# A two-branch cross-attention kernel on one core: the list scheduler's durations, switch penalties and ranks set anew

## The chip, the cores and the metric

The kernel runs on one core of a Trainium2 chip. A core has a matrix engine (TensorE, PE in the profile), a vector engine (DVE), an activation engine (ACT), a general engine (GpSimd, POOL) and an engine that here issues transfers only (SyncE, SP). Each works through its own list of instructions in order; they wait for one another by semaphores. The metric is the device time of one execution in microseconds. The kernel before took 582.35 us, the median of three runs (582.03 to 583.09).

## The reference, cut to what matters

```python
# x (2, 2048, 640) float32, ctx_768 (2, 128, 384); 8 heads of 80; the last T = 4 context rows are "ca"
query = x @ Wq;  keyt = enc @ Wk;  valt = enc @ Wv         # enc: the other 124 context rows
hs = _mha(query, keyt, valt)                               # text branch
ca_q1 = einsum('btc,th->bch', ca, Wq_ca)[:, indices, :]    # 2048 rows picked from 384
ca_hs1 = _mha(ca_q1, x, x)                                 # adapter: 384 distinct queries over 2048 rows
ca_q2 = ca_hs1 @ Wq
ca_hs2 = _mha(ca_q2, ca @ Wk_ca, ca @ Wv_ca)
out = (hs + ca_hs2) @ Wout + b_out + x
```

## The kernel before, in words

*Two branches.* The text branch makes the queries q of 512 rows of x at a time (eight blocks: four for each of two batches), the scores sc against the 124 keys, a softmax (row maximum m on DVE, exponential p with its row sum on ACT, a reciprocal r, the product p<-p,r), a transposition in blocks (eb on DVE, a store kept<-eb to device memory and four loads pT<-kept), then the products ph with the values (copied to hs), and po with Wout, which DVE adds to the rows of x (x_more, last_rows). It does this in 16 units (m) of 256 rows. The adapter branch makes, for each batch, small products of x (pyz, copied to yz, turned into y and zop), the first scores s1 (24 products of four row tiles into the one score buffer of four banks, each followed by a maximum mx on DVE), a shift of the queries by these maxima (mt, cop), the second scores s2 (24 products, each followed by an exponential ea on ACT), the contraction acc of ea with y, its normalisation (accs, prod, the second small softmax p2) and the product po with w_sb into 384 rows o2 in device memory. At the end of a unit each of its two row tiles gets its o2 rows added by an indirect DMA on POOL (`add_second`) and is stored. Products by Strassen-like sums (x_sums, wq_sums, wout_sums, sums of hs) save matmuls at the price of additions on DVE and POOL.

*Tilings of PE.* A matmul may use part of the array: column tiles (128*32 in the profile, four beside one another), row tiles for the scores s (32*128), halves for sc (64*128), quarters for pyz (64*32), and the whole array for transposes and the set-up (128*128). `matmul` is line 210 of the profile, `by_columns` 222, `transpose` 230, the operations of the other engines 245, `dma` 265; all operations go through these helpers, so the groups are known by tile names.

*The planner.* The order is not written out. Each piece of the kernel is a generator (`softmax`, `adapter`, `probabilities`, `chain` inside `text_out`, and so on) that yields `Do` entries: an engine (or several to choose from, `EITHER`), what must be done first, buffers it needs (`Room`) and frees, a rank, and a tiling mode. `Desk.run` keeps a clock of its own while the program is built: for every engine it finds the earliest time at which an entry could start, takes among the entries of that time the one with the lowest rank plus penalty for changing PE's tiling, issues it, and adds its assumed duration. `Desk.pin` then keeps that order on each engine in the finished program. So durations, penalties and ranks decide only two things: the order on each engine, and the engine of an operation that may go to several (copies to ACT or DVE; p<-p,r to POOL, DVE or ACT; sums of x, hs and wout to DVE or POOL). `RANKS` adds a number to the rank of single generators, by name and count. `MORE`, `START`, `DRAIN`, `TAIL` and the third argument of each `dma` call are assumed durations in microseconds. Column-tile products are entered as the whole array (`mode=(P, P)`), scores without a mode.

*Events and counters.* Some buffers are given back by counting the users that are done (`used`, `counted`, `scored`, `left`), at the moment when the planner issues the last. The output has a path for rows that are done before o2 is there (`stored`: a part to device memory and back, with the room `ending`); in the program that is built, no row takes that path, and 30 stores of whole rows and four of halves end the kernel.

Of the kernel before, what the change touches and what calls it, by code (L numbers as in the profile page):

```python
# [14 lines left out]
P = 128  # L15
# [49 lines left out]
class Desk:  # L65
# [4 lines left out]
    WHOLE, SWITCH, LEAVE, ANOTHER = (P, P), 328.5, 9.9, 185.7  # L70
    START = {(P, P): 0.107, (64, P): 0.143, (P, 64): 0.107, (64, 32): 0.1, (P, 32): 0.03}
    DRAIN = {
        ((P, P), (32, P)): 0.136, ((P, P), (64, P)): 0.035, ((P, P), (P, 64)): 0.056, ((P, P), (P, 32)): 0.067,
        ((32, P), (P, 32)): 0.049, ((P, 64), (P, P)): 0.07, ((P, P), (P, P)): 0.0,
    }
    DRAINS = {(64, P): 0.172, (32, P): 0.108, (P, 32): 0.115}
    MORE = {
        "v_transpose": 0.025, "v_stream_shuffle": 0.09, "v_scalar_tensor_tensor": 0.07, "v_reciprocal": 0.035,
        "a_activation": 0.045,
    }  # L80
    COLD = 5.2
    TAIL = {"PE": 0.25, "DVE": 0.18, "ACT": 0.2, "POOL": 0.25, "SP": 0.1, "NONE": 0.0}
# [3 lines left out]
        "adapter": {0: 1, 1: 2},  # L86
        "chain": {2: 8, 4: -11, 5: 7, 6: -2, 8: -11, 11: -4, 14: 11, 15: 16, 19: -14, 24: -4, 25: 3, 30: 3.1,
            32: 4, 34: 10, 36: 2, 41: 0.5, 42: 1, 43: 0.5, 44: -10, 45: -10, 48: -8, 50: -5, 51: -5, 52: 7,
            54: 10, 55: 10, 56: 10, 68: -4, 76: -3, 81: 2, 86: 2, 87: 3},
        "contract": {0: 5, 1: 4.5, 2: 8, 3: 8},  # L90
        "halves_away": {1: -4, 2: -2, 4: 4, 6: 6},
        "keys": {0: -10},
        "probabilities": {3: -8, 5: -4, 8: 12, 9: -3, 10: -2, 12: 6, 13: 6, 15: 7},
        "queries_fast": {0: 5, 3: 4},
        "rest_back": {1: 11, 4: 5, 7: 8, 9: 9, 10: 5, 14: 2},
        "second": {0: 2.3},
        "softmax": {0: 5, 2: -7, 3: 6.2, 4: -4, 7: -11, 8: 2, 10: -5, 12: -20, 14: -3, 17: 9, 20: -2, 21: 7,
            22: 7, 25: -5, 29: 2, 30: 6},
        "sums_of_wq": {0: 5.7},
        "text_scores": {0: -8, 1: 3.4, 12: 9},  # L100
        "values_weights": {0: -18},
        "x_load": {1: 4.2, 4: 5},
        "y_rows": {2: 2, 3: 6, 4: 4},
        "y_weights": {0: 1},
        "yz_block": {2: 16, 5: 3.5, 6: 5},
    }

    def __init__(self, tc):
        self.tc, self.nc, self.now, self.spent, self.mode = tc, tc.nc, 0.0, 0.0, None
        self.free = {e: 0.0 for e in self.ENGINES}  # L110
        self.queue = {e: [] for e in self.ENGINES}
        self.events, self.landed, self.channel, self.log, self.begun = {}, 0.0, 0.0, [], {}

# [29 lines left out]
    def change(self, mode):  # L143


        if mode is None or mode == self.mode:
            return 0.0
        return self.LEAVE if self.mode == self.WHOLE else self.SWITCH if mode == self.WHOLE else self.ANOTHER
# [17 lines left out]
    def run(self):  # L166
        while any(self.queue.values()):
            best = None
            for e in self.ENGINES:
                found = [(max(r, self.free[e], self.now), op) for op in self.queue[e] if (r := self.ready(op)) is not None]  # L170
                if found:
                    t = min(x[0] for x in found)
                    t, op = min(
                        (x for x in found if x[0] <= t + 1e-9),
                        key=lambda x: self.order(x[1]) + self.change(x[1].mode),
                    )
                    if best is None or t < best[0]:
                        best = t, e, op
# [23 lines left out]
    def _mode(self, rows, cols):  # L202
        mode = tuple(32 if n <= 32 else 64 if n <= 64 else 128 for n in (rows, cols))
        if mode != self.mode or self.idle:
            self.spent += self.START.get(mode, 0.0)
            self.spent += self.DRAIN.get((self.mode, mode), self.DRAINS.get(self.mode, 0.1))
        self.mode, self.idle = mode, False

    def matmul(self, out, lhsT, rhs, **kw):
        self.pin(self.nc.tensor.matmul(out, lhsT, rhs, **kw))  # L210
        n = 1
        for size in rhs.shape[1:]:
            n *= size
# [3 lines left out]
        self.spent += self.slow() * (1 if one else 2) * max(n / 1.2, 107) / 1e3 / at_once  # L217

    def by_columns(self, out, lhsT, rhs, **kw):
# [3 lines left out]
        n = 1  # L223
        for size in rhs.shape[1:]:
            n *= size
        self._mode(P, P)
        self.spent += 2 * max(n / 1.2, 107) / 1e3

    def transpose(self, out, in_, ident):
        self.pin(self.nc.tensor.transpose(out, in_, ident))  # L230
        self._mode(P, P)
        self.spent += self.slow() * 0.115
# [30 lines left out]
    def dma(self, out, in_, us, issue=0.45, more=2.8):  # L263

        self.pin(self.nc.sync.dma_start(out, in_))
        self.spent += issue
        self.channel = max(self.channel, self.now + self.spent) + us
        self.landed = self.channel + more


@with_exitstack
def kernel(
# [56 lines left out]
    ending, early, late = Room(1), Room(0), {}  # L329
# [570 lines left out]
    def keys():  # L900
# [39 lines left out]
        for i in range(2):  # L940
            op = yield Do(
                "SP", lambda i=i: dma(away[:, :, i].rearrange("e p n -> p e n"), z.bitcast(F32), 0.8), rank=-1,
            )
        for u in range(2):
            for e in range(2):

                def back(u=u, e=e):
                    dma(
                        parts[VH * u + G * e : VH * u + G * (e + 1)],
                        away[e, VH * u : VH * (u + 1)].rearrange("(g d) i n -> (d i) g n", g=4), 0.4,  # L950
# [37 lines left out]
    def load_wout():  # L988

        by_head = Wout.rearrange("(c j d) n -> j d c n", c=4, j=2)  # L990
        for j in range(2):
            yield Do(
                "SP", lambda j=j: dma(wout_sb[VH * j : VH * (j + 1), :4, :], by_head[j, :VH], 2.5),
# [3 lines left out]
        def last():  # L997
            for h in range(HEADS):
                dma(wout_sb[VR * h : VR * (h + 1), 4, :], Wout[D * h + VH : D * (h + 1), :], 0.15)
# [126 lines left out]
    def x_load(b, sb, after):  # L1126
# [8 lines left out]
        for i in range(4):  # L1135
# [3 lines left out]
            def of_pairs():  # L1139
                d1 = VR + (R * i + VH) % P  # L1140
                dma(most[part, :2], v[:, 0::2, :, d0 : d0 + R], 2.2, 1.3)
# [4 lines left out]
            def between_pairs():  # L1146
                if i:
                    g = (0, 2, 1, 3)[i]
                    dma(rest[part], w[:, :, D2 * g - VR : D2 * g + VR], 0.6, 0.6)
                else:  # L1150
                    dma(rest[part, :, :VR], w[:, :, H - VR :], 0.6, 0.6)
                    dma(rest[part, :, VR:], w[:, :, :VR], 0.6, 0.6)
# [26 lines left out]
    def queries(n, after, first=False):  # L1179
# [8 lines left out]
        if first:  # L1188
# [53 lines left out]
            used(b, sb, op)  # L1242
            yield Do("NONE", lambda: None, [("qc", n, j, h) for j in range(2) for h in range(2)], marks=[("q", n)])
            return
        for c in range(NCH):
# [10 lines left out]
            op = yield Do("PE", part, [*after, "wq4"], needs=[(banks, 1), *own], mode=(P, P))  # L1256
            pq, s, q = op.value, op.slots[0][0], q_of[n][0]

            for i0, i1 in ((2, 4), (4, NCH)):
# [5 lines left out]
                op = yield Do("PE", part, mode=(P, P))  # L1265
# [4 lines left out]
        used(b, sb, op)  # L1270
# [6 lines left out]
    def sums_of_wq():  # L1277
# [3 lines left out]
        yield Do("NONE", lambda: None, ["late"])  # L1281
# [39 lines left out]
    def queries_fast(n, after):  # L1321

        sb = divmod(n, NSB)
        yield Do("NONE", lambda: None, after + ["late"])
# [12 lines left out]
        left = {"all": 9, "sums": 4}  # L1337
        rank = 10 + 2 * n

        def counted(op, of_sums):  # L1340
            left["all"] -= 1
            left["sums"] -= of_sums
            if of_sums and not left["sums"]:
                if n + 1 < len(blocks):
                    sums.at[0] = op.at.t
                else:
                    desk.event("last sums").t = op.at.t
            if not left["all"]:
                used(*sb, op)
                if n + 1 == len(blocks):  # L1350
                    desk.event("last query").t = op.at.t

        def chain(c, steps):

            po, s, at = None, None, []
            for k, ((x, y, plus), ready, (i, u)) in enumerate(steps):
# [20 lines left out]
                if x is not None:  # L1377
                    needs = ([(banks, 1)] if k == 0 else []) + ([(qslots, 1)] if n not in q_of else [])
                    op = yield Do("PE", product, ready + at, needs=needs, mode=(P, P))
# [7 lines left out]
                if plus:  # L1387
                    op = yield Do("PE", fifth, [op.at] + at, mode=(P, P))
                counted(op, any(key[0] == "xs" for key in ready))
# [21 lines left out]
        yield from plain(n, t, NCH - 1, rank - 0.5, counted)  # L1411
# [8 lines left out]
    def plain(n, t, c, rank, counted):  # L1420
# [7 lines left out]
        op = yield Do("PE", part, needs=[(banks, 1)], mode=(P, P), rank=rank)  # L1428
        pq, s = op.value, op.slots[0][0]
        for i0, i1 in ((2, 4), (4, NCH)):  # L1430
# [5 lines left out]
            op = yield Do("PE", part, mode=(P, P), rank=rank)  # L1436
        counted(op, False)
        yield Fork(halves_away(n, pq, s, op.at), 0)

    users = {}  # L1440
# [953 lines left out]
```

## Time and profile before

| | |
|---|---|
| median of three runs | 582.35 us |
| profiled execution, its device time | 581.8 us |
| its span | 580.1 us |
| PE busy | 570.3 us (98%) |
| DVE busy | 391.7 us (68%) |
| ACT busy | 309.8 us (53%) |
| POOL busy | 141.6 us (24%) |
| DMA moved | 112.71 MB |
| granted clock of PE | 1.000 |

Spans and starts are those of the one profiled execution. In a list of groups a line gives the helper's line, the engine, the operation, the tiles out<-in, the number of instructions, then busy us and the mean ns of one, then the idle time of that engine just before them. Instructions overlap a little on PE, DVE and ACT: start-to-start is shorter than the recorded duration. In the slices each digit is a tenth of 14.5 us.

### The profile page before, as it was taken

Reading aid. Unit: us, or ns where it says so; the run is one execution under the profiler, and the core shown is the slowest. Engines: PE = TensorE matmul, PEld = TensorE weight load, DVE = VectorE, ACT = ScalarE, POOL = GpSimd, SP = SyncE. Lnnn points to the kernel's source line nnn. Section 1 sums busy time; section 2 is a strip of 40 time slices with the busy share of each in tenths; the row PEclk is TensorE's granted clock in tenths of the full one; section 3 lists DMA queues with packets and bytes.
Section 4 is the critical chain, followed back from the end, with each engine's and each line's share of the span. In section 5 each row is a group of like instructions: output and inputs, shape, how many; then the busy total and the mean of one; then the engine's idle time right before and its main releaser. Section 6 shows DMA issues by size and latency. Waiting matters only on the chain.

```text
span 580.1 us, 19105 instructions
## 1 busy us (share of the span) xinstructions
PE 570.3 (98%) x8115; PEld 308.4 (53%) x8115; DVE 391.7 (68%) x645; ACT 309.8 (53%) x869; POOL 141.6 (24%) x200
## 2 busy tenths in 40 slices
PE   9999999999999999999999999999999999999997
PEld 8885334555555545455455445454455545545453
DVE  2446799999999756356999999973455253444443
ACT  2413376686566898689847447277877613002020
POOL 9102112012206411120114326050140312403241
PEclk9999999999999999999999999999999999999999
DMA  8897866979766888234999969999549487799995
GB/s 245 196 263 131 199 94 187 179 201 172 182 184 137 217 157 221 82 113 149 219 284 247 230 152 236 270 227 275 142 105 266 112 211 155 181 263 247 250 249 139
DMA packets 153039, 112.71 MB, mean 194 GB/s; under 512 B 83701, under 2 KB 126581, under 8 KB 152954
## 3 DMA queue, kind: packets, MB, share of 16 engines
q1 hardware_dynamic: 147322, 100.80, 67.5%
q0 software_dynamic: 5632, 10.69, 11.3%
q8 instruction: 64, 1.05, 0.8%
q14 instruction: 21, 0.17, 0.1%
HBM read 71.23 MB, written 40.22 MB: 192 GB/s over the span
## 4 chain that ended last, share of the span: by engine, by line
PE 64%; DVE 16%; DMA 8%; ACT 6%; issue 4%; SPq 1%; DVEq 0%; ACTq 0%
PE po L222 25%; PE pq L222 9%; PE ph L210 6%; DVE mx L245 6%; PE acc L210 5%; PE s L210 4%; PE pq L210 4%; PE sc L210 3%; ACT ea L245 3%; DMA kept<-eb 3%; DMA pT<-kept 2%; ACT p L245 2%; DVE m L245 2%; DVE q L245 2%; DVE eb L245 2%
## 5 line engine op out<-in xcount | busy, mean ns | idle before, releaser
L245 DVE TENSOR_REDUCE mx<-s 128x4 f32<-128x2048 f32 x48 | 109.4, 2280 | 4.1 <-PE s L210 4.1
L245 ACT ACTIVATE ea<-s 128x2048 f32<-128x2048 f32 x48 | 91.0, 1897 | 24.2 <-PE s L210 23.9
L245 ACT ACTIVATE p<-sc,m 128x124 f32<-128x124 f32 x256 | 90.2, 383 | 10.2 <-DVE m L245 9.7
L222 PE MATMUL po<-wout_sums,hs 128*32 128x320 f32 x1024 | 77.3, 433 | 0.0
L222 PE MATMUL po<-wout_sb,hs 128*32 128x320 f32 x960 | 74.2, 433 | 0.7 <-DVE x_more L245 0.7
L222 PE MATMUL pq<-xt,wq_sb 128*32 128x256 f32 (+1 forms) x928 | 66.3, 418 | 0.5 <-DVE mt L245 0.5
L245 DVE TENSOR_TENSOR x_more<-x_more,po 128x320 f32<-128x320 f32 x72 | 34.3, 483 | 45.5 <-PE po L222 45.4
L2129 POOL DMA_INDIRECT x_more<-o,query x18 | 27.9, 1550 | 124.3 <-DVE x_more L245 92.5
L245 ACT ACTIVATION_READ_ACCUMULATOR p<-sc,m 128x1 f32 x256 | 57.8, 226 | 0.0
L245 ACT COPY hs<-ph 128x512 f32<-128x512 f32 (+1 forms) x34 | 18.5, 551 | 65.8 <-PE ph L210 65.2
L222 PEld LDWEIGHTS po<-wout_sums,hs 128*32 128x32 f32 x1024 | 32.9, 110 | 34.1 <-issue 1.8
L210 PE MATMUL acc<-ea,y_sb 128*32 128x384 f32 (+2 forms) x768 | 51.0, 385 | 0.0
L222 PEld LDWEIGHTS po<-wout_sb,hs 128*32 128x32 f32 x960 | 30.4, 110 | 33.1 <-issue 1.5
L245 DVE TENSOR_REDUCE m<-sc 128x4 f32<-128x496 f32 x64 | 40.0, 662 | 10.4 <-PE sc L210 10.4
L245 DVE TENSOR_TENSOR last_rows<-last_rows,po 128x320 f32<-128x320 f32 x56 | 26.7, 481 | 27.9 <-PE po L222 27.5
L210 PE MATMUL ph<-pT,vpad 128*32 128x256 f32 x768 | 45.3, 380 | 0.1
L245 POOL TENSOR_TENSOR p<-p,r 128x992 f32<-128x992 f32 x8 | 14.8, 1846 | 125.0 <-DVE r L245 125.0
L222 PEld LDWEIGHTS pq<-xt,wq_sb 128*32 128x32 f32 x928 | 27.8, 109 | 29.6 <-issue 13.5
L245 DVE STREAM_TRANSPOSE eb<-p 128x1024 f32<-128x1024 f32 x32 | 39.4, 1233 | 5.6 <-DMA kept<-eb 5.5
L210 PEld LDWEIGHTS sc<-kmain,q 64*128 64x128 f32 x512 | 32.1, 187 | 13.7 <-issue 5.5
L210 PE MATMUL sc<-kmain,q 64*128 64x124 f32 x512 | 38.4, 285 | 0.2 <-ACT p L245 0.2
L245 ACT CAST rests<-landing 128x512 fp32r<-128x512 f32 x30 | 18.7, 635 | 36.2 <-PE sc L210 28.0
(216 smaller groups left out, 847.6 us busy)
## 6 DMA issues: line engine op xcount, KB each, us to landing
kept<-eb SPq DMA_DIRECT2D x32, 512.0 KB, 3.8
pT<-kept SPq DMA_DIRECT2D x64, 256.0 KB, 8.2
landing<-away SPq DMA_DIRECT2D x60, 128.0 KB, 4.3
xi<-in_x_dram SPq DMA_DIRECT2D x56, 128.0 KB, 4.6
x_more<-in_x_dram SPq DMA_DIRECT2D x18, 320.0 KB, 6.8
out_dram<-x_more SPq DMA_DIRECT2D x16, 320.0 KB, 6.6
last_rows<-in_x_dram SPq DMA_DIRECT2D x14, 320.0 KB, 7.2
out_dram<-last_rows SPq DMA_DIRECT2D x14, 320.0 KB, 10.0
```

The costliest lines, as they stand in the source:

```text
L210: self.pin(self.nc.tensor.matmul(out, lhsT, rhs, **kw))
L222: self.pin(self.nc.tensor.matmul(out[j : j + 32], lhsT[:, j : j + 32], rhs, **kw))
L245: self.pin(getattr(engine, what)(*args, **kw))
L2129: desk.pin(nc.gpsimd.indirect_dma_start(out=t, out_offset=None, in_=o2_of[b], in_offset=bass.IndirectOffsetOnAxis(ap=query[:, st : st + 1] ...
```

## The change

All of it lies in the planner and in the bookkeeping that feeds it; each operation computes what it did. The penalties for changing the tiling now depend on both modes (`CHANGE`; letters b for column tiles, s for row tiles of the scores, c for sc, y for pyz, w for the whole array), and column tiles and scores are entered with their own modes. The price of a PE stretch is set by `ENTER`, `EXIT` and `streamed`. An entry that could start later than the earliest one carries a penalty `IDLE`; `AHEAD` (0) is the width of that choice. A transfer now takes one of eight places in flight per queue in the planner (`SLOTS`, `transfer`): a ninth is issued when the first has landed. Each `dma` call has a new assumed duration, and some a new issue time and latency. Buffers are given back by events (`free_x`, `free_q`, `done`, `sum`, `chain` marks) in place of counters. The path over device memory for early rows is gone. `RANKS` grows from some 60 entries to several hundred.

```diff
-    WHOLE, SWITCH, LEAVE, ANOTHER = (P, P), 328.5, 9.9, 185.7
-    START = {(P, P): 0.107, (64, P): 0.143, (P, 64): 0.107, (64, 32): 0.1, (P, 32): 0.03}
...
+    KINDS = {(P, 32): "b", (32, P): "s", (64, P): "c", (64, 32): "y", (P, P): "w"}
+    CHANGE = {
+        "bs": -2.82893e+09, "bc": 34.1, "by": 7.8, "bw": 66.5, "sb": 2.7632e+10, "sc": 659476, "sy": 6.8, "sw":
+        16.2, "cb": 486.2, "cs": 12, "cy": 3.3, "cw": 21.1, "yb": 609.7, "ys": 0.8, "yc": 12, "yw": 9.2, "wb":
+        6379.5, "ws": 14.8, "wc": 27.3, "wy": 16.5,
     }
-    DRAINS = {(64, P): 0.172, (32, P): 0.108, (P, 32): 0.115}
+    AHEAD, IDLE = 0, 214.8
+    ENTER = {(P, P): 0.104, (64, P): 0.143, (64, 32): 0.16, (P, 32): 0.024, (32, P): 0.006}
+    EXIT = {(P, P): 0.07, (P, 32): 0.114}
+    SLOTS = 8
...
-    TAIL = {"PE": 0.25, "DVE": 0.18, "ACT": 0.2, "POOL": 0.25, "SP": 0.1, "NONE": 0.0}
+    TAIL = {"PE": 0.235, "DVE": 0.14, "ACT": 0.145, "POOL": 0.16, "SP": 0.1, "NONE": 0.0}
...
     RANKS = {
-        "adapter": {0: 1, 1: 2},
...
+        "adapter": {0: 37.7, 1: 41.7, 3: 1},
...
-                    t = min(x[0] for x in found)
+                    first = min(x[0] for x in found)
+                    ahead = self.AHEAD if e == "PE" else 1e-9
                     t, op = min(
-                        (x for x in found if x[0] <= t + 1e-9),
-                        key=lambda x: self.order(x[1]) + self.change(x[1].mode),
+                        (x for x in found if x[0] <= first + ahead),
+                        key=lambda x: self.order(x[1]) + self.change(x[1].mode) + self.IDLE * (x[0] - first),
                     )
...
+    def streamed(self, rhs):
+        n = 1
+        for size in rhs.shape[1:]:
             n *= size
+        return (max(n / 1.2, 106 if self.mode[1] > 32 else 27) + (9 if self.mode == (64, P) else 2.5)) / 1e3
...
-        self._mode(P, P)
-        self.spent += 2 * max(n / 1.2, 107) / 1e3
+        self._mode(P, 32)
+        self.spent += 2 * self.streamed(rhs)
...
-    def dma(self, out, in_, us, issue=0.45, more=2.8):
+    def dma(self, out, in_, us, issue=0.47, more=3.0):
 
         self.pin(self.nc.sync.dma_start(out, in_))
-        self.spent += issue
+        self.transfer("SP", us, issue, more)
+
+    def transfer(self, side, us, issue, more=3.0):
+
+        flights = self.flights[side]
+        self.spent = max(self.spent, flights.pop(0) - self.now) + issue
         self.channel = max(self.channel, self.now + self.spent) + us
         self.landed = self.channel + more
+        flights.append(self.landed)
...
-                    op = yield Do("PE", scores, [("zop", b, sb, u), c_at], needs=[(quad, 1)])
+                    op = yield Do("PE", scores, [("zop", b, sb, u), c_at], needs=[(quad, 1)], mode=(32, P))
...
-                lambda: dma(pT[R * j : R * (j + 1)].rearrange("p i k h a -> p i (k h a)"), by_keys[j], 1.1),
+                lambda: dma(pT[R * j : R * (j + 1)].rearrange("p i k h a -> p i (k h a)"), by_keys[j], 1.2, 0.48),
...
-                "SP", lambda: dma(o2_of[b][ct * P : (ct + 1) * P, :], o2, 1.3),
+                "SP", lambda: dma(o2_of[b][ct * P : (ct + 1) * P, :], o2, 1.1, 0.39),
...
-        desk.spent += 1.9
-        desk.landed = desk.now + desk.spent + 6.5
+        desk.transfer("POOL", 1.5, 1.57)
...
-            part = hbm.tile([P, H], F32, tag=f"early_{m}_{k}", name=f"early_{b}_{st}")
-            op = yield Do("SP", lambda: dma(part, t, 1.3), both, frees=[(rows, i)])
...
+        op = yield Do("POOL", lambda: add_second(t, b, st), [*both, ("o2", b), "query"])
+        yield Do("SP", lambda: dma(rows_out, t, 1.3, 0.41), frees=[(rows, i)])
```

More of the change, by code (lines that the diff above doesn't have):

```diff
@@ L1255, in queries @@
             own = [(qslots, 1)] if n not in q_of else []
-            op = yield Do("PE", part, [*after, "wq4"], needs=[(banks, 1), *own], mode=(P, P))
+            op = yield Do("PE", part, [*after, "wq4"], needs=[(banks, 1), *own], mode=(P, 32))
             pq, s, q = op.value, op.slots[0][0], q_of[n][0]
@@ L1323, in queries_fast @@
         sb = divmod(n, NSB)
-        yield Do("NONE", lambda: None, after + ["late"])
+        yield Do("NONE", lambda: None, after + ["late", "wq sums"])
         t, _ = xt[sb]
@@ L2265, in chain @@
-                tile_left[m, i] = tile_left.get((m, i), 4) - 1
-                ends.setdefault((m, i), []).append(op.at)
-                if not tile_left[m, i]:
-                    yield Fork(stored(m, i, ends[m, i]), 1)
+        reads = {(i, u): [] for i in range(2) for u in range(2)}
+        for n, steps in enumerate(chains):
+            for _, _, (place,) in steps:
+                reads[place].append(("sum", m, *place, n))
+        yield Fork(one(Do(
+            "NONE", lambda: None, [("chain", m, n) for n in range(len(chains))], frees=[(hss, at_hs)]
+        )), 0)
```

274 lines of the change are left out of this document (139 added, 135 removed), and 14 rows, old and new, of the table RANKS.

## The prediction

> **What bounds the kernel now.** I read the page first, then the busy times by stretch, then what TensorE (PE) waited for. The page:
>
> ```profile
> PE 570.3 (98%) x8115; PEld 308.4 (53%) x8115; DVE 391.7 (68%) x645; ACT 309.8 (53%) x869; POOL 141.6 (24%) x200
> ...
> PE   9999999999999999999999999999999999999997
> ...
> DVE  2446799999999756356999999973455253444443
> ACT  2413376686566898689847447277877613002020
> ...
> PEclk9999999999999999999999999999999999999999
> ```
>
> PE is busy in every slice and its granted clock never drops. DVE is full twice (slices 5 to 13 and 20 to 24), ACT nearly so between them and around slice 28. The span is 580.1 us and the profiled run 581.8, so 1.7 us lie around it; that run is 0.55 us under the median of 582.35. The busy time of the engines in stretches (stretch, length, then PE, PEld, DVE, ACT, POOL, clock, DMA share, GB/s):
>
> ```profile
> 20.00:110.00 90.00, 89.97 (x931) 50.02 (x932) 68.84 (x121) 40.33 (x131) 11.59 (x41) 1.00 0.79 168
> 110.00:190.00 80.00, 79.02 (x1218) 43.33 (x1214) 77.68 (x103) 55.47 (x212) 21.19 (x24) 1.00 0.76 175
> 190.00:290.00 100.00, 97.64 (x1523) 51.65 (x1519) 62.62 (x102) 83.88 (x201) 15.91 (x16) 1.00 0.66 166
> 290.00:345.00 55.00, 53.96 (x799) 27.84 (x795) 53.88 (x59) 29.82 (x114) 16.25 (x14) 1.00 0.91 234
> 345.00:410.00 65.00, 64.47 (x974) 32.62 (x966) 47.87 (x69) 38.78 (x103) 21.14 (x19) 1.00 0.97 246
> 410.00:470.00 60.00, 59.97 (x952) 31.57 (x945) 28.05 (x56) 42.29 (x75) 10.75 (x12) 1.00 0.63 153
> 470.00:580.10 110.10, 106.38 (x1643) 54.32 (x1642) 45.99 (x99) 13.85 (x28) 29.25 (x19) 1.00 0.86 213
> ```
>
> PE stands idle 0.98 + 2.36 + 1.04 + 0.53 = 4.9 us between 110 and 410 us, and almost nothing at 20 to 110 and 410 to 470. The last 3.72 us are the final addition and stores. So a reordering can win those 4.9 us, the price of PE's changes of tiling, and what is hidden inside "busy". What PE waited for (us, times, longest):
>
> ```profile
> PE s L210 <- ACT ea L245: 1.6, 6, 0.5
> PE unread L210 <- DVE zeros L245: 1.1, 1, 1.1
> PE s L210 <- DVE mx L245: 0.8, 2, 0.5
> PE po L222 <- DVE x_more L245: 0.7, 2, 0.5
> PE pq L222 <- DVE mt L245: 0.5, 1, 0.5
> ```
>
> The largest are the second scores s, which wait until ACT has taken the exponential ea out of the one score buffer, and the first scores, which wait for DVE's maximum mx.
>
> **The change, part by part.** The arithmetic stays: both programs issue the same 4520 matmuls, so PE's streaming costs the same and has no term. What moves is the order on each engine, and which engine takes the operations that two or three may take. Counts of the new program are read from its issue order; their durations are the rows of before.
>
> *Changes of tiling.* The planner adds a penalty to an operation that would change PE's tiling, and the change sets these penalties anew. Stretches of equal tiling go from 270 to 267; those that leave the column tiling (128*32), from 112 to 109. Other kinds keep their numbers. One such departure:
>
> ```profile
> 35.40 1.08 PE L210 MATMUL pa<-first_rows,blk_k 128*32 128x128 f32 x32
> 36.30 0.40 PE L210 MATMUL pa<-wqT,blk_k 128*32 128x128 f32 x8
> 36.63 1.16 PE L210 MATMUL pa<-first_rows,blk_k 128*128 128x128 f32 x8
> ```
>
> Eight groups of four take 36.30 - 35.40 = 0.90 us, 0.1125 each. Two more would end at 36.525; the next tiling starts at 36.63, so leaving cost 0.105 us here (0.137 over all departures that I could place like this). Three fewer: 3 x 0.137 = -0.4 us. Bounds: 0 and -0.4.
>
> *Stages.* For each stage I compared PE's work without waiting with the work of the engine that limits it, start to start. The rows:
>
> ```profile
> L245 DVE TENSOR_REDUCE mx<-s 128x4 f32<-128x2048 f32 x48 | 109.4, 2280 | 4.1 <-PE s L210 4.1
> L245 ACT ACTIVATE ea<-s 128x2048 f32<-128x2048 f32 x48 | 91.0, 1897 | 24.2 <-PE s L210 23.9
> ...
> L245 DVE TENSOR_TENSOR x_more<-x_more,po 128x320 f32<-128x320 f32 x72 | 34.3, 483 | 45.5 <-PE po L222 45.4
> ...
> L245 DVE TENSOR_REDUCE m<-sc 128x4 f32<-128x496 f32 x64 | 40.0, 662 | 10.4 <-PE sc L210 10.4
> ...
> L245 DVE STREAM_TRANSPOSE eb<-p 128x1024 f32<-128x1024 f32 x32 | 39.4, 1233 | 5.6 <-DMA kept<-eb 5.5
> ```
>
> ```profile
> 310.94 2.28 DVE L245 TENSOR_REDUCE mx<-s 128x4 f32<-128x2048 f32 x1
> 313.14 1.24 DVE L245 STREAM_TRANSPOSE eb<-p 128x1024 f32<-128x1024 f32 x1
> ```
>
> ```profile
> 198.25 0.36 ACT L245 ACTIVATE p<-sc,m 128x124 f32<-128x124 f32 x1
> ...
> 198.59 0.36 ACT L245 ACTIVATE p<-sc,m 128x124 f32<-128x124 f32 x1
> ```
>
> A full DVE starts the next instruction 0.08 us before the recorded end (310.94 + 2.28 - 313.14), so I take 0.08 off each; an exponential p with its read-out costs ACT 0.34.
>
> Stage A, the first scores of batch 0 (to about 167 us). DVE's 140 instructions make 120.1 us beside 118.6 of PE; after, 137 make 117.6 beside 115.4. The excess goes from 1.5 to 2.2 us. Read alone, +0.7; the bound below is that all 0.98 of its idle time goes. I take 0: stages overlap, so an excess of this size can move out of the stage.
>
> Stage B, the second scores of batch 0 (181 to 264 us). ACT has 74.5 us beside 82.9 of PE; after, 85.0 beside 92.2. The room shrinks from 8.4 to 7.2 us in a longer stage, as 24 more of the normalisations p<-p,r go to ACT in all (104 to 128, that is three units more). But the score loop gets looser: a score buffer is free again 1.9 us plus two hand-overs after a product, so the other PE work between two second-score products should be about 2.2 us or more. Of the 47 gaps, those below 2.2 us go from 8 to 3, those below 2.55 from 16 to 7. With PE's 1.6 us of waits for ea spread over six places, I take a third to a half of them gone, -0.6. Bounds: -2.4 (the idle time of 190 to 290 gone) and +1.2 (if ACT does all its work as soon as its inputs are there, its worst lateness goes from 1.04 to 2.22).
>
> Stage C, the first scores of batch 1 (266 to 357 us). DVE has 93.1 us beside 91.2 of PE: 24 mx x 2.20 = 52.8, 16 m x 0.58 = 9.3, 24 additions to rows x 0.40 = 9.6, 8 eb x 1.15 = 9.2, and 12.2 of others. After, it has 100.7 beside 101.6: seven more additions and three copies of hs, but 10.4 us more of PE products, so an excess of 1.9 becomes a room of 0.9. The idle time of 290 to 410, 1.04 + 0.53, holds x_more's 0.7 and one mx. I take -1.3; bounds -1.6 and 0.
>
> *Transfers.* The planner now lets a ninth transfer of a queue wait for the first's landing; the chip is given no wait, only another order. Reuse of the output rows in the tail loosens (shortest distance 28 to 33 us), and one stall of the chain below, x_more's, hangs on such a load. -0.3; bounds -0.7 and 0. One place tightens. The pT of unit 0 is now issued on SP right behind the store o<-o, which waits for ACT's copy of a product; from that product to the first ph that needs this pT lie 10.4 us of PE work (16.1 at the tightest place before). The rows of such a group, of its landing, and two links of the chain of waits:
>
> ```profile
> 308.26 0.34 SPq L265 DMA_DIRECT2D o<-o  x1
> ...
> 309.54 1.84 SPq L265 DMA_DIRECT2D pT<-kept  x4
> ```
>
> ```profile
> DMA to landing us min/median/max: 3.5/8.2/11.5
> ```
>
> ```profile
> 316.64 8.04 DMA x_more<-in_x_dram
> 324.69 5.86 DMA pT<-kept
> ```
>
> The copy came about 1.2 us after its product. With 1.2 + 0.4 for the store, some 1.4 to the fourth issue of 1.84, and 8.2 to land, pT is there 11.2 us after the product: 0.8 late. Behind SP's waiting entry queue the loads after it, with ten us of cover each. I take +0.5 (PE's own small waits lengthen the cover); bounds 0 and 4.1 (landing 11.5).
>
> *Other moves.* Five copies of hs and two or three of q go from ACT to DVE where DVE is at four tenths to half busy (slices 25 to 33), so at nothing: in the second scores of batch 1 (369 to 445 us) DVE has 31.8 us of work beside 75.7 of PE. Without that cover a copy would cost the 0.69 us of its row less 0.08. Three sums of hs go from DVE to POOL, and in stage A POOL takes five instead of three of the p<-p,r. Rows that bear on these:
>
> ```profile
> L245 DVE TENSOR_TENSOR x_sums<-xt x3: 676/677/1741, 74.8 to 254.9; 128x512 f32<-128x512 f32 x3
> ```
>
> ```profile
> L245 DVE COPY hs<-ph x4: 640/686/693, 381.1 to 432.1; 128x512 f32<-128x512 f32 x4
> ```
>
> ```profile
> L245 POOL TENSOR_TENSOR p<-p,r x8: 1845/1846/1848, 95.2 to 309.9; 128x992 f32<-128x992 f32 x8
> ```
>
> DVE's sum of two rows takes 677 ns, but once 1741, so two-input work on DVE can stretch by 1.06 us; POOL's product never stretched. I price the two moved products at 0: POOL is a quarter busy and p is needed late. If each of the two held up DVE once in stage A, that is +2.1 us. The Trainium skill says, in "SBUF — State Buffer", section "Who interferes with whom", that a DVE instruction with two SBUF inputs and a GpSimd instruction that reads SBUF share one port pair as an exclusive lock, and the later one waits for the whole of the other; it speaks against these moves. The row of 1741 agrees in sign; the sum by that rule would be 2.1 us higher.
>
> *The sum.* -0.4 + 0 - 0.6 - 1.3 - 0.3 + 0.5 = -2.1 us, so 581.8 - 2.1 = 579.7 on the scale of the profiled run and 580.25 on that of the median. I say 580.0.
>
> **The rivals.** *Nothing but the tiling changes moves.* If DVE and ACT each did all their work as soon as its inputs are there, the latest operand of each stage would be late by amounts that sum to about 4.2 us in both orders; the stalls would then only change places. Against it: the places over 0.25 us late fall from 58 to 34. Then 582.35 - 0.4 = 582.0.
>
> *Most stalls go.* All of 190 to 410's 3.9 us and the switches: 582.35 - 4.3 = 578.0, and with as much again that hides inside "busy" (by the start-to-start of undisturbed products, PE took about 8 us longer there than its streams and tiling changes), down to 574.5. For it: the looser loops. Against: ACT's room in B shrinks.
>
> *Slower: pT of unit 0 lands late.* The cover of 10.4 us less the 3.0 before the last issue leaves 7.4 to land; the case decides at 7.4 plus the 2.6 that the other terms win, a landing of 10.0. At 345 to 410 us transfers take 97% of the DMA engines, and the slowest pT took 11.5; should the new order bring that crowd to 305 us, the stall is 4 to 6 us, and the time 580.0 - 0.5 + 4 to 6 = 583.5 to 585.5. The Trainium skill adds in "TensorE: Matmul & The Clock Gate", Part 1, that about 3.4 us of idle PE sends it to half its clock. No wait of PE in before is over 1.1 us and its clock stays full, so no run here shows that yet.
>
> *Slower: ACT or the shared reads bound A and B.* A at +0.7 in place of 0, B at +1.2 in place of -0.6, and the two products' 2.1: 580.0 + 0.7 + 1.8 + 2.1 = 584.6. For it: stage A has more DVE than PE, so what is lost there isn't hidden. Against: 1741 stands once.
>
> **How the numbers follow.** The forecast 0.42, its own range 578.5 to 581.2; most stalls go 0.17; nothing moves 0.15; pT late 0.13; ACT or shared reads 0.13. Within 0.2% of 582.35 (581.2 to 583.5, what a measurement here can tell from no change) lies the second of these: same 0.15, faster 0.59, slower 0.26. The range 575 to 585 takes in most of every case.
>
> **What would show it.** Right: PE's waits for ea and mx below 1.6 and 0.8 us, for x_more none; idle time at 190 to 290 below 2 us and in stage C near 0. The switches: 109 departures from 128*32. Wrong: a wait of ph for pT near 300 to 320 us over 1 us; DVE sums over 1.5 us in stage A; an idle time of 3 us or more at 180 to 270 us with releaser ea. The forecast falls, too, if landings, which the planner takes as fixed, lengthen in the new order and new waits appear where no term above stands.

## The result, and the profile after

The changed kernel takes 587.73 us (median of five, 585.32 to 588.40); the kernel before, run beside it, 582.03 (five, 581.37 to 583.09). The ratio is 1.0089, with a 95% interval of 1.0064 to 1.0114: it is slower by 0.9%. The profiled execution took 587.91 us with a span of 585.9. One execution of a later run (the maximum first) fell into a slower state, 721.84 us at a mean clock of 0.754, and is left out of that run's median.

The page of the kernel after, its busy times and three of the lines of slices (40 equal slices, tenths busy or, for PEclk, of full clock):

```profile
PE 570.0 (97%) x8115; PEld 309.1 (53%) x8115; DVE 398.6 (68%) x653; ACT 311.2 (53%) x881; POOL 139.2 (24%) x201
...
PE   8999999999989999899999999999999999999997
...
DVE  1456999999798836855699999996633314445343
...
PEclk9999999999989999999999999999999999999999
```

PE's work is the same; PE's busy time and its clock both have a dent in the twelfth slice (161 to 176 us), which the kernel before had not. By stretches (columns as before the change: length, then PE, PEld, DVE, ACT, POOL, clock, DMA share, GB/s):

```profile
0.00:20.00 20.00, 17.71 (x104) 15.88 (x105) 6.14 (x34) 4.75 (x8) 15.48 (x59) 1.00 0.84 260
20.00:110.00 90.00, 90.00 (x915) 50.08 (x917) 69.95 (x130) 36.29 (x111) 12.13 (x41) 1.00 0.82 175
110.00:190.00 80.00, 75.61 (x1130) 40.91 (x1130) 73.51 (x99) 53.81 (x217) 16.88 (x13) 0.98 0.78 174
190.00:290.00 100.00, 97.35 (x1603) 54.71 (x1591) 65.61 (x102) 86.50 (x211) 17.71 (x25) 1.00 0.59 159
290.00:345.00 55.00, 53.03 (x771) 27.67 (x760) 51.77 (x64) 32.12 (x121) 9.65 (x10) 1.00 0.84 232
345.00:410.00 65.00, 64.49 (x950) 33.47 (x946) 58.46 (x77) 37.35 (x131) 23.48 (x21) 1.00 0.88 237
```

PE's idle time at 110 to 190 us went from 0.98 to 4.39 us, and the clock there fell to 0.98, some 1.6 us of 80: together 5.0 us in this one stretch, where the span grew by 5.8 in all. At 190 to 290 the idle time is 2.65 for 2.36, at 290 to 410 it is 2.48 for 1.57. The 2.29 for 1.14 at the start is one late load of x; the runs below that keep this order up to 100 us show 1.13 to 1.16. Against these stands PE's busy time, which includes its changes of tiling: it is 568.1 to 569.1 us in the five later runs whose clock stays at 1.00, and 570.3 before. PE's waits (us, times, longest):

```profile
PE s L266 <- DVE mx L295: 3.4, 3, 2.2
PE s L266 <- ACT ea L295: 2.0, 2, 1.2
...
PE pq L275 <- ACT p L295: 0.8, 1, 0.8
PE pq L275 <- DVE prod L295: 0.7, 1, 0.7
PE s L266 <- DVE zop L295: 0.7, 1, 0.7
```

One wait of 2.2 us for a maximum is new. DVE's instructions ahead of it (start, us, what, and idle time before with its releaser):

```profile
152.94 1.25 DVE L295 STREAM_TRANSPOSE eb<-p 128x1024 f32<-128x1024 f32 x1 [1.05 <-DMA kept<-eb]
...
158.14 0.67 DVE L295 TENSOR_TENSOR q<-q,pq 128x512 f32<-128x512 f32 x1
160.87 1.25 DVE L295 STREAM_TRANSPOSE eb<-p 128x1024 f32<-128x1024 f32 x1 [2.06 <-DMA kept<-eb]
162.31 0.01 DVE L295 LOAD_MASK_SELECT zs<-yz  x1 [0.20 <-DMA z<-zs]
...
164.12 2.29 DVE L295 TENSOR_REDUCE mx<-s 128x4 f32<-128x2048 f32 x1
```

The full engine stood still for 1.05 and 2.06 us. There is one buffer eb; its next transposition waits until the store kept<-eb has landed, and behind that transposition stood a maximum whose scores PE had finished soon after 158 us. The store was late on SP. SP's transfers (start, us of issue):

```profile
145.78 0.54 SPq L315 DMA_DIRECT2D y_sb<-y  x1
146.36 0.64 SPq L315 DMA_DIRECT2D xi<-in_x_dram  x1
147.05 0.67 SPq L1198 DMA_DIRECT2D xi<-in_x_dram  x1
147.76 0.98 SPq L315 DMA_DIRECT2D xi<-in_x_dram  x1
148.83 0.56 SPq L315 DMA_DIRECT2D kept<-eb  x1
149.44 0.64 SPq L315 DMA_DIRECT2D xi<-in_x_dram  x1
150.12 1.19 SPq L1198 DMA_DIRECT2D xi<-in_x_dram  x1
151.36 2.29 SPq L315 DMA_DIRECT2D y_sb<-y  x1
153.69 0.43 SPq L315 DMA_DIRECT2D xi<-in_x_dram  x1
154.22 1.86 SPq L315 DMA_DIRECT2D landing<-away  x4
156.13 0.42 SPq L315 DMA_DIRECT2D y_sb<-y  x1
156.66 0.57 SPq L315 DMA_DIRECT2D kept<-eb  x1
```

The transposition that filled eb ended at 145.0; its store was issued at 148.83, behind loads of x that are first transposed at 166 us. The next one, on which the wait of 2.06 us hung, ended at 154.2, and its store was issued at 156.66, behind a load of x, four loads of landing and one of y_sb. SP issues with no pause over 0.42 us from 134.9 to 159 us. What followed the wait, in short stretches:

```profile
164.00:166.50 2.50, 0.26 (x8) 0.04 (x4) 2.50 (x3) 2.50 (x14) 0.00 (x0) 1.00 0.63 227
166.50:169.00 2.50, 2.50 (x28) 2.26 (x28) 2.50 (x5) 1.85 (x9) 0.00 (x0) 0.78 0.00 0
169.00:171.00 2.00, 2.00 (x14) 0.57 (x17) 2.00 (x3) 1.67 (x6) 0.00 (x0) 0.50 0.00 0
171.00:173.00 2.00, 2.00 (x40) 0.91 (x32) 1.98 (x4) 1.34 (x6) 0.00 (x0) 0.93 0.62 174
```

After 2.24 us without a product the granted clock fell to a half: 0.22 x 2.5 + 0.50 x 2.0 + 0.07 x 2.0 = 1.7 us more, which at a half is some 3.4 us of lowered clock. Not every execution shows it: of the five, three have a mean clock of 0.994 to 0.996 (587.73 to 588.40 us) and two of 1.000 (585.32 and 586.95). Only the one of 587.91 was traced, so whether those two had the stall is not known.

### The profile page after: what moved, and what is told of

It reads as the page before. It is cut to its first block, busy times and chain, and to the rows that moved or that the text cites. A ratio compares the mean times of both kernels' runs of the same rounds, so it can differ in the third digit from the quotient of the medians.

```text
span 585.9 us, 19137 instructions
## 1 busy us (share of the span) xinstructions
PE 570.0 (97%) x8115; PEld 309.1 (53%) x8115; DVE 398.6 (68%) x653; ACT 311.2 (53%) x881; POOL 139.2 (24%) x201
## 3 DMA queue, kind: packets, MB, share of 16 engines
q8 instruction: 64, 1.05, 0.8%
## 4 chain that ended last, share of the span: by engine, by line
PE 77%; DVE 10%; DMA 6%; ACT 3%; issue 2%; SPq 1%; POOL 1%; DVEq 0%; ACTq 0%
PE po L275 25%; PE pq L275 17%; PE acc L266 7%; PE ph L266 6%; PE s L266 6%; PE sc L266 5%; PE pq L266 4%; DVE mx L295 3%; PE pyz L266 2%; DMA pT<-kept 1%; DVE m L295 1%; ACT p L295 1%; DMA x_more<-o,query 1%; PE pv L266 1%; PE pk L266 1%
## 5 line engine op out<-in xcount | busy, mean ns | idle before, releaser
L295 DVE TENSOR_TENSOR last_rows<-last_rows,po 128x320 f32<-128x320 f32 x68 | 32.6, 483 | 45.9 <-PE po L275 45.5
L295 ACT ACTIVATION_READ_ACCUMULATOR p<-sc,m 128x1 f32 x256 | 55.8, 218 | 0.0
L295 DVE TENSOR_TENSOR x_more<-x_more,po 128x320 f32<-128x320 f32 x60 | 28.7, 480 | 35.7 <-PE po L275 34.0
L2183 POOL DMA_INDIRECT last_rows<-o,query x17 | 26.3, 1546 | 97.8 <-DVE last_rows L295 73.9
L266 PE MATMUL ph<-pT,vpad 128*32 128x256 f32 x768 | 46.7, 380 | 0.4 <-DMA pT<-kept 0.2
L295 ACT COPY hs<-ph 128x512 f32<-128x512 f32 (+1 forms) x29 | 15.5, 546 | 57.4 <-PE ph L266 57.2
L295 ACT ACTIVATE p<-p,r 128x124 f32<-128x124 f32 x128 | 38.9, 395 | 13.1 <-DVE r L295 13.0
```

What stands on the lines that cost most here:

```text
L295: self.pin(getattr(engine, what)(*args, **kw))
L2183: desk.pin(nc.gpsimd.indirect_dma_start(out=t, out_offset=None, in_=o2_of[b], in_offset=bass.IndirectOffsetOnAxis(ap=query[:, st : st + 1] ...
```

## The experiments

In all but three of the runs the planner's choice is replaced by a list: the 2353 entries of the changed kernel's own plan, with their buffers, are issued in that order, and only the entries named are moved. Without an edit the list is the changed kernel's own order. So an edit moves what it names and nothing else is decided anew. "Less" is against the changed kernel's 587.73.

**The stall of 2.2 us, from three sides.** First, stores ahead on SP:

```diff
 SP:
+ kept<-eb                      (issued at 148.8 us)
  xi<-in_x_dram x3              (146.4 to 148.8)
- kept<-eb
...
+ y_sb<-y, kept<-eb, y<-yt, z<-zs   (156.1 to 159.0)
  landing<-away x4                  (154.2 to 156.1)
- y_sb<-y, kept<-eb, y<-yt, z<-zs
```

> The order of the changed kernel is held fixed as a list; on SP two loads of x and four loads of the rests step behind three stores (kept<-eb twice, z<-zs) around 146 to 159 us. Theory A: in the first scores DVE has no room, and the stall of 2.24 us before the score at 166.46 us comes from DVE waiting, in its fixed order, for these stores to land; the half clock after it (about 1.7 us) comes from the stall. Then the stall is under 0.5 us, the clock is 1.00 in the stretch 166 to 173, and the run takes 3 to 4 us less than the changed kernel's 587.9, some 584. Rival: DVE is simply overfull in this stage, the stall moves to the next maximum, and the time stays within 1 us of 587.9.

Measured: 587.83 us, nothing won, though the wait of 2.2 us for mx went (the longest left is 0.8). The chip answered with another wait (PE, then ACT):

```profile
PE pq L491 <- ACT q L511: 4.3, 2, 4.1
```

```profile
162.25 0.62 ACT L511 CAST rests<-landing 128x512 fp32r<-128x512 f32 x1 [10.29 <-DMA landing<-away]
162.78 0.58 ACT L511 COPY q<-pq 128x512 f32<-128x512 f32 x1
```

ACT, too, works in a fixed order: its cast of rests stood ahead of a copy of q, and the four loads of landing had been put back by the edit. Neither theory had this. For DVE the first survives in part: its waits for stores fell from 3.3 us to 1.2 (0.80 for eb, 0.35 for zs). The crowd on SP hit the engine that waits for the transfer put last. Second, DVE's order with SP's left alone:

```diff
 DVE:
- eb<-p, zs<-yz                 (160.9 to 163.0 us)
  m<-sc x2
  mx<-s                         (164.1)
+ eb<-p, zs<-yz
```

> SP's order stays that of the changed kernel; on DVE one block transposition eb and one shuffle zs step behind the maximum mx that stood behind them at 164.12 us. Theory A: the maximum had its input since about 159 us and stood behind two waits for stores, so it now runs at about 160 to 162 us, the score comes without the 2.24 us stall and the clock stays full: 3 to 4 us less than 587.9. Rival (DVE is overfull): the later transposition pushes the next maximum by the same amount and less than 1 us is won.

Measured: 583.34 us, 4.4 less; 1.0027 of the kernel before (1.0013 to 1.0042). DVE and the clock (the last column but two) in this run:

```profile
157.48 1.23 DVE L511 TENSOR_REDUCE m<-sc 128x4 f32<-128x496 f32 x2
158.65 2.27 DVE L511 TENSOR_REDUCE mx<-s 128x4 f32<-128x2048 f32 x1
160.85 1.21 DVE L511 STREAM_TRANSPOSE eb<-p 128x1024 f32<-128x1024 f32 x1
162.00 0.00 DVE L511 LOAD_MASK_SELECT zs<-yz  x1
```

```profile
166.50:169.00 2.50, 1.74 (x31) 0.71 (x20) 2.50 (x5) 2.25 (x8) 0.00 (x0) 1.00 0.24 64
169.00:171.00 2.00, 1.81 (x36) 1.12 (x40) 2.00 (x3) 2.00 (x11) 0.00 (x0) 1.00 0.79 254
```

The store has landed by the time that DVE comes to this eb, DVE does not stop there (0.27 us is left of the earlier wait), and the clock stays whole. Third, SP again, without the mistake of the first run: the loads of x go back, not those that ACT waits for.

```diff
 SP:
- xi<-in_x_dram, four steps     (146.4 to 154.1 us)
  kept<-eb, y_sb<-y, landing<-away x4, y_sb<-y
  kept<-eb, y<-yt, z<-zs
+ xi<-in_x_dram, four steps
```

> The changed kernel's order with one edit on SP alone: four steps of loads of x for the fifth block (issued from 146 to 154 us, first transposed at 166 us) step behind the stores kept<-eb, y<-yt and z<-zs of 157 to 158 us; the loads of the rests, which ACT waits for, keep their place ahead of the stores. If SP's crowd of transfers is the cause of DVE's two waits for stores (1.05 and 2.06 us), these and the 2.24 us stall of PE go with DVE's order unchanged, no new wait on ACT appears, and the time is 583 to 584.5. If the crowd is only one of several things late here, the stall moves as it did in the first run of this kind, and the time stays above 586.

Measured: 583.49 us, 4.2 less; 1.0038 of the kernel before (1.0020 to 1.0057). DVE's order is that of the changed kernel here:

```profile
151.86 1.19 DVE L511 STREAM_TRANSPOSE eb<-p 128x1024 f32<-128x1024 f32 x1
...
157.59 1.22 DVE L511 STREAM_TRANSPOSE eb<-p 128x1024 f32<-128x1024 f32 x1
```

Both waits for stores are gone with SP's order alone. Two smaller ones came: 0.80 us of DVE for the loads that were put back, and 1.43 us of PE for ACT's copy of q at 169 to 170 us, which the expectation had excluded. Either side of the wait, moved alone, wins about the same, 4.4 and 4.2 us. That settles the largest part of the 5.7.

**Sums beside sums.** In the changed kernel DVE's zop at 110.70 us took 1.77 us, while POOL did its sums of x (109.21 to 111.9), and the addition of wq_sb before it 1.19. To tell the neighbour from the place:

```diff
 DVE:
+ zop, wq_sb<-wq_sb x2, zs      (109.6 to 113.4 us)
  xt<-xi x2                     (108.4; POOL's sums wait for these)
- zop, wq_sb<-wq_sb x2, zs
```

> On DVE the two additions of wq_sb, zop and zs around 110 us step ahead of the two transpositions of xt that release POOL's sums of x. Theory A: the 1.77 us of zop (0.71 elsewhere) and the 1.19 us of wq_sb (0.41 elsewhere) come from running beside POOL's sums; ahead of them they take 0.7 and 0.4 us, PE's waits of 0.65 and 0.77 us at 112 and 115 us go, and the time falls by 1.4 to 1.8 us to about 586.3. Rival: the long zop has another cause (its position), keeps its 1.77 us, and nothing is won.

Measured: 589.32 us, slower by 1.6. DVE in this run:

```profile
108.25 0.73 DVE L511 SCALAR_TENSOR_TENSOR zop<-zop,low_z,zs 128x512 fp32r<-128x512 f32 x1
108.90 0.76 DVE L511 TENSOR_TENSOR wq_sb<-wq_sb 128x256 f32<-128x256 f32 x2
```

Away from POOL's sums zop takes 0.73 us and the two additions 0.76 together (1.19 + 0.41 before). PE's idle time at 100 to 120 us went from 1.42 to 0.00, as expected. But the loads of the next block of x start 1.85 us later, since xt is read later, and 1.96 us come back as idle time at 120 to 140. That is 0.5 us more idle time, not 1.6. The stall of 2.2 us is still there too, now 2.31 us long and ending at 167.00, and behind it the clock stayed lowered for longer than in the changed kernel:

```profile
167.00:169.50 2.50, 2.50 (x23) 2.25 (x24) 2.50 (x5) 1.85 (x9) 0.00 (x0) 0.62 0.00 0
169.50:171.50 2.00, 2.00 (x18) 1.21 (x19) 2.00 (x2) 1.71 (x6) 0.00 (x0) 0.50 0.00 0
171.50:174.00 2.50, 2.50 (x27) 0.94 (x20) 1.82 (x4) 1.34 (x6) 0.00 (x0) 0.50 0.50 157
```

That loses 3.4 us in this execution, where the changed kernel's lost 1.7. So the cause of the long zop is shown, its neighbour on POOL; that moving it away costs 1.6 us by itself is not, since the clock may have made most of that. A milder edit, on top of the run with the maximum first, leaves xt in its place:

```diff
 DVE:
  xt<-xi x2
+ m<-sc x2, zop
  wq_sb<-wq_sb x2, zs
- zop, m<-sc x2
```

> The order of the run with the maximum first, and on DVE the two reductions m and zop ahead of the two additions of wq_sb at 109.6 us, so that reductions from the score banks, not sums of two rows, run beside POOL's two sums; the transpositions of xt and with them the loads of x stay where they are. Theory (shared reads): the wq_sb addition of 1.19 us and the zop of 1.77 us shrink by 0.7 to 1.8 us together, PE's wait of 0.77 us at 115 us goes, and the run takes 0.7 to 1.4 us less than the 583.5 of the run with the maximum first. Rival: the loads of x set the pace here, as the run with zop ahead of xt showed, and nothing is won.

Measured: 582.75 us, and 1.0001 of the kernel before (0.9988 to 1.0014): the changed kernel's deficit is gone with two edits. It is 0.6 less than the 583.34 of the run that it stands on, and the two intervals overlap, so the second edit's share is not clear of noise. The two additions fell to 0.75 us together, zop still took 1.68, and DVE's work shrank by 0.9 us. PE's wait at 114 us, 0.78 us in the run with only the maximum first, did not go (1.01), so a gain at PE is not shown.

**The second scores.** Two ea ahead of the p whose place they took:

```diff
 ACT:
+ ea<-s                         (229.7 us; and again at 237.4)
  p<-sc,m x2                    (x4 the second time)
- ea<-s
```

> On ACT two exponentials ea of the second scores, at 229.73 and 237.42 us, step ahead of two and four exponentials p whose place they took. Theory A: these stalls (0.74 and 1.21 us) were in the plan's order and go, since the score was ready 0.7 and 1.4 us before ea began: 1.5 to 2 us less than 587.9, about 586.2. Rival: the p made later hold up the next products sc or the maxima, and less than 0.5 us is won.

Measured: 587.22 us, 0.5 less, which lies within the changed kernel's own spread (585.32 to 588.40). The two waits for ea, 0.74 and 1.21 us, shrank to one of 0.18, and PE's idle time at 180 to 290 us fell from 2.65 to 1.64 us. New waits are small (0.34 us of sc for ACT's yz, 0.22 of acc for an ea), but PE was busy 9.42 us with 137 products between 230 and 240 us where it had been 8.04 with 140, so that little of the gain arrived; why is not shown. The time fits the rival, and ACT is full here (10.00 of these 10 us); a pure stall of order it was not.

**All of it together.** Three edits on top of the run with m first (five in all), then a variant with the costly one replaced:

```diff
 DVE:   wout_sums<-wout_sb,wout_sums behind mx       (second run: given to POOL)
 PE:    pt_p<-ident,p2pad one product later
 ACT:   q<-pq ahead of wq_sums<-pq                   (first run)
 ACT:   ea<-s at 229.7 us ahead of two p             (second run)
```

> As the last, and in addition: DVE's sum wout_sums at 313.2 us (1.79 us beside POOL's sums) behind the maximum that it delays; the transpose pt_p on PE one product later; the copy of q on ACT ahead of one cast. If each of PE's waits there goes (0.87, 0.5 and 0.3 us), the run takes 1.7 us less than the last, some 580.5 to 581, and beats the kernel before. If the stages are tied, each win comes back as a new wait within 20 us and the time stays at that of the last.

> The order of the run with m first, and in addition: DVE's sum wout_sums of 313 us is given to POOL (in the last run its delay on DVE cost 1.69 us at a sum of hs behind it on POOL); pt_p on PE one product later; of the two exponentials ea of the second scores only the one at 229.73 us steps ahead of its p (the other brought its 1.5 us back as new waits). If each holds alone, 0.87 + 0.58 + 0.79 us go from the 582.75 of the run with m first: 580.5, below the kernel before. If the stages are tied, no less than 582.

Measured: 584.03 us (1.0025, 1.0008 to 1.0042) and 583.06 us (1.0020, 1.0007 to 1.0033). In the first, DVE's wout_sums, which took 1.79 us beside POOL's sums, took less than half behind them, and PE's wait of 0.8 us for the maximum fell to 0.24; but sums of hs on POOL stood behind it:

```profile
316.61 0.82 DVE L511 TENSOR_TENSOR wout_sums<-wout_sb,wout_sums 128x640 f32<-128x640 f32 x1
```

```profile
PE po L491 <- POOL hs L511: 1.7, 1, 1.7
```

In the second it is POOL's work that makes the same hs late, by 1.0 us. What was won at the maximum came back at POOL; neither run beats the kernel before, and none of the edits that I tried makes a version that does.

**Durations or ranks.** These three runs let the planner decide again. Its own clock, which it keeps while the program is built and which is no measurement, is given beside each.

```diff
-    RANKS = { ... }
+    RANKS = {}
```

> The kernel before with an empty table of ranks: its durations and penalties alone set the order. The planner's own clock ends at 615.9 us here (595.2 with the ranks, where the chip took 582). If its durations are simply too long by about 2%, the chip takes some 603 us. If a searched table alone brings the chip under the plan, it takes 616 or more.

> The changed kernel with an empty table of ranks: its new durations and penalties alone. The planner's own clock ends at 609.6 us here (574.7 with the ranks, where the chip took 587.7, 13 us more). Theory S (the search has used up every slack that the durations show, so any lateness on the chip is paid): without the search the plan is loose and the chip takes 609 to 615 us, at most 5 more than the plan. Rival (the new durations are simply too short): the chip again takes 13 us or more over the plan, 622 us or later.

```diff
-    SLOTS = 8
+    SLOTS = 99
```

> The changed kernel with one constant of the planner undone: 99 places in flight per queue instead of 8, all ranks as they are. The planner's own clock ends at 619.5 us instead of 574.7. If the table of ranks is fitted to one exact plan, the chip takes more than 605 us; if the ranks hold something of the kernel itself, it stays near 588.

```
                              planner's clock    chip, us    chip less plan    lowered clock
kernel before                      595.2           582.0        -13.2              0.0
  without ranks                    615.9           606.4         -9.5              3.4
changed kernel                     574.7           587.7        +13.0              1.7
  without ranks                    609.6           615.7         +6.1              8.0
  with SLOTS = 99                  619.5           626.1         +6.6             10.0
```

The last column is an estimate from each profiled execution: PE's busy time in steps of half a microsecond, times what the granted clock lacked in that step. Over the span the clock was 0.992 in the kernel before without ranks, 0.977 and 0.970 in the last two rows. The planner has no term for a lowered clock after its first 5.2 us. With that taken out, both orders of the old durations end some 13 us before their plans, and the new durations without ranks 1.9 us before theirs: old durations were too long, so that the old plan's steps were ready early on the chip, and nothing here shows that the new ones are too short. With the ranks the chip is 11.3 us late on the new plan. That speaks for Theory S, though the chip took 0.7 us more than it allowed. Off the old plan the search took 20.7 us, and 21.0 arrived; off the new it took 34.9, and 21.7 arrived (28.0 with the clock). The ranks belong to one plan: with one constant changed the same ranks give 626.1 us (one run), 10 more than no ranks at all. Whether the new durations give worse orders in general isn't shown; without ranks there is one order of each. The same maxima in plan and trace show where it slips (start of the n-th mx, planned / measured):

```
 n        1            12             13             18             21             24
before  54.3/53.2   112.4/108.7    118.5/114.6    150.0/145.0    165.6/160.1    180.2/174.4
after   54.8/56.1   105.6/106.2    112.2/114.5    142.9/144.9    158.6/164.1    173.0/179.2
```

Before, the chip gains on the plan throughout. After, it loses 1.7 us between the 12th and 13th (zop beside POOL's sums) and 3.5 between the 18th and 21st (the stores). SP is later than DVE: the store of 143.05 us in the plan was issued at 148.83, when DVE was 2.0 late; single issues there took 2.1 to 2.3 us where 0.5 to 0.6 was assumed.

## Why the prediction was wrong

580.0 us was forecast, with 575 to 585 as the range; 587.7 came. By the steps:

*Stage A, "I take 0"*, is the step that failed: it cost 5.0 us in the profiled execution, of which the stall of 2.24 us and the lowered clock behind it make 3.9; moving one side of that wait won 4.2 to 4.4. DVE's work was counted, but DVE was taken as an engine that is never idle. It waits in order for two buffers, eb and zs, whose release is a landing, and the path of that landing over SP was not followed. The prediction followed SP's order only at pT and the output rows, though its own row for eb shows DVE idle for 5.5 us before it, released by kept<-eb. In the kernel before these waits stood at 387 to 405 us, where PE stayed busy (25.00 of the 25 us from 380 to 405).

A late store alone was not new. In the kernel before one was issued 4.3 us after its transposition (136.31 to 140.60 us), but the next transposition came at 147.13. In the changed kernel the lags were 3.8 and 2.5 us, but its plan put these transpositions 8.1 and 5.8 us apart (141.71, 149.79 and 155.64), less than a transposition of 1.2, the lag and a landing of 3.9 take together. The distance that mattered was from one eb to the next, against the place of the store between them in SP's queue.

*Changes of tiling*, -0.4: three fewer, as counted (267 stretches, 109 departures). PE's busy time fell by more, 1.2 to 2.2 us in the five runs whose clock stays whole; how much of that is tiling is not shown.

*Stage B*, -0.6: the waits for ea went from 1.6 us at six places to 2.0 at two, the idle time of 190 to 290 from 2.36 to 2.65. Fewer and longer; nothing won. That ACT sets this stage was right.

*Stage C*, -1.3: +0.9 at 290 to 410 us. DVE was busy 110.2 of the 120 us (101.8 before); x_more's waits fell from 0.7 to 0.3. But one maximum came 0.8 us late behind wout_sums, which took 1.80 us beside POOL's sums.

*Late transfers*, -0.3: they moved nothing that can be read apart. *pT of unit 0*, +0.5: ph began at 315.32 us without a wait; the one wait of ph for pT, 0.2 us, is another unit's. This rival was wrong.

*Shared reads* were in the text as a rival with 2.1 us, at 0.13 together with ACT. DVE's instructions with two inputs did stretch beside POOL's sums: zop took 1.77 us for 0.73, wout_sums 1.80 for 0.82, and each ended 0.6 to 0.7 us after POOL's sum did. This agrees with the Trainium skill, "SBUF — State Buffer", section "Who interferes with whom", by which a DVE instruction with two SBUF inputs contends with a GpSimd instruction that reads SBUF. But the pairs were others than the two products that were priced. PE's waits beside them were 0.65 and 0.77 us in A and 0.8 in C, and the runs that took them away were not faster.

*The clock.* The forecast put the half clock only behind a late pT, with the idle time of about 3.4 us that the Trainium skill gives in "TensorE: Matmul & The Clock Gate", Part 1. In the profiled execution 2.24 us were enough, and the measurement decides.

The last sentence of the prediction named half of what happened: new waits appeared where no term stood. The landing itself did not lengthen much (kept<-eb lands 3.9 us after its issue, 3.8 before); what the new order left no room for was the time until the issue. The root of the mistake was to sum up terms for the stalls that were there, with none for stalls that a tighter order makes.

## What to carry to other kernels

When a planner writes the order, compare its clock with the trace before believing a better plan: here the search won some 21 us on the chip with either set of durations and penalties, the lowered clock taken out, and what it won beyond that on the shorter ones stayed on paper. The runs suggest, but do not show, that the longer durations were the slack that made the old order hold. For an engine that is full, list the buffers that its instructions wait for, and follow each to the end, through the queue of its store, and set that time against the distance to the next user; a single buffer with a store behind prefetching loads can be a stall that no count of work shows. An edit that removes a wait is only a gain if what it pushes back has room of its own; in at least half of the edited runs here it had none.

## What the runs showed of the hardware that was not expected

PE's clock fell to a half after 2.24 us without a product and stayed there for some 3.4 us; the same followed 2.19 us in the run with ea first and 4.07 us in the first run (0.50 and 0.70 in the four us after), while after 2.31 us in the run with zop first it lasted some 6.8 us. Gaps of 1.43 us (loads behind) and 1.69 us (the first of all together) left it at 1.00. The length of a single gap does not decide: in the kernel before without ranks a gap of 1.34 us, half a microsecond after one of 0.57, was followed by a clock of 0.50, and one of 1.77 us left it at 1.00. And two of the changed kernel's five executions show a mean clock of 1.000.

An issue on SP, in the stretch shown mostly 0.43 to 0.67 us, took 2.1 to 2.3 us at single places within a crowd; the kernel before has one of 2.24 us too (at 122.56). Why, these runs leave open.

And a DVE instruction with two inputs in SBUF took up to 2.9 times as long beside a POOL sum (wq_sb, 1.19 us for 0.41), also as SCALAR_TENSOR_TENSOR (1.77 us for 0.73).
